# Sixteen adjacency-mask pieces moved from the first projection into the first attention of a four-layer graph network

## The chip, the cores and the metric

The kernel runs on one core of one Trainium2 chip. A core has a matrix engine (TensorE, PE in the profile, with its weight loads as PEld), a vector engine (VectorE, DVE), an activation engine (ScalarE, ACT), a general engine (GpSimd, POOL) and a queue engine (SyncE, SP). Each of them [...] waits on semaphores for the others. Transfers between the memory of the chip and the core's SBUF are issued by SP, ACT or POOL. The metric is the device time of one execution in microseconds (us), and the median of several executions is compared.

## The reference

The input is x, 3327 rows of 512 numbers, and adj, a 3327 x 3327 integer matrix of zeros and ones. Four layers follow one another, each closed by `x = layernorm(x + layer(x, adj))`. Layers 0, 2 and 3 are graph attentions. For a head with projected rows `Wh` and two scalars per row, f1 and f2,

```
e         = leaky_relu(f1[:, None] + f2[None, :], 0.2)
attention = softmax(where(adj > 0, e, -9e15), axis=-1)
h_prime   = attention @ Wh
```

Layers 0 and 2 have 8 heads of 64, layer 3 has 4 heads of 128. Layer 1 takes, for each row, the mean over its first 64 neighbours and two linear maps. The matrix adj is the same in all four layers.

## The kernel before

The rows are cut into NT = 26 tiles of 128 (NP = 3328), and the columns of the attention (the rows i that are being computed) into two halves of 1664. The adjacency matrix is given transposed. It is turned once into a mask of 8-bit floats that stays in SBUF for all four layers: `mask[:, t, i]`, one row tile t of neighbours against all i. This is done in 104 pieces of 128 x 832, four per row tile: q = 0 and 1 cover the first half of i, q = 2 and 3 the second. A piece is a transfer of 416 KB of integers into a buffer `raw` (L628) and one instruction that compares it with zero: on VectorE a `tensor_scalar` (L639), or on ScalarE a steep sigmoid (L638). `pieces` (L1103) lists first q = 0, 1 for every tile, then q = 2 for every tile, then q = 3.

The first stage is the projection of layer 0 (L1132 to L1154). For each row tile t, the rows of x are loaded (`xt`, issued on POOL after the first three), PE turns them (L266, four transposes), ScalarE copies the result out, and PE multiplies it with the weights (L276, 16 instructions into two PSUM banks `pw`, of which each has two buffers). VectorE then sums the turned rows (L268) and scales the product into `vt` (L282), which releases the PSUM bank and is stored to memory by POOL (L288). In this loop the mask is begun as well: `msteps` (L1105) is a list of steps for the first EARLY = 68 pieces, with eight `raw` buffers, eight loads on the queue of ScalarE and the rest on SP, and a lag of five steps between loading a piece and setting it. Three or four of these steps are taken per row tile (L1143). All 68 are set by VectorE.

The second stage is the attention of layer 0. It consists of 8 units: two halves times four slots s of two heads each. A unit goes over the 26 row tiles j. For each j and each of its two heads, VectorE makes `t` (L410, 128 x 1664), ScalarE makes `y` from it (L413), and PE multiplies `t` with the values `vj` (L433, 16 instructions per j) and, two tiles later and for two tiles at once, `y` and the mask with small matrices for the denominators (L385). There are six buffers of `t` and seven of `y`. Once per j two lists are served (L438 to L441): `background`, which holds the leftovers of the unit before (transposes L461 of its result) and jobs such as the neighbour counts (`count_jobs`, L658) or the small products `pa` of the later layers' weights (L1122); and `aside`, which holds the steps of the remaining mask pieces: load one, set the one before. The pool for these has two `raw` buffers, and the loads go through SP. In the kernel before, the 36 pieces that remain take 37 steps, so the first unit and eleven tiles of the second. ScalarE sets those with k % 5 in (1, 3), which are 14; VectorE sets 22.

The second half of the mask is first needed by the neighbour counts of the second half, in the third unit (half 0, s = 2), and by the attention from the fifth unit on. The instructions of PE stand in the order of the program. Those of the other engines are put in order by a scheduler, except for single ones that are pinned; the mask instructions of the attention are pinned.

Of the kernel before, what the change touches and what calls it, by code (L numbers as in the profile page):

```python
# [32 lines left out]
def kernel(  # L33
# [12 lines left out]
    NT = (N + P - 1) // P  # L46
# [575 lines left out]
    def mask_load(pool, t, q, eng):  # L622
        n = P if t < NT - 1 else LAST
        i0 = q * QW
        w_ = min(QW, N - i0)
        raw = pool.tile([P, QW], I32, name="raw")
        for a, z in _row_pieces(n):
            eng.dma_start(out=raw[a:z, :w_], in_=adjT[t * P + a:t * P + z, i0:i0 + w_])  # L628
        return raw

    def mask_set(raw, t, q, on_act=False):
        n = P if t < NT - 1 else LAST
        i0 = q * QW
        w_ = min(QW, N - i0)
        dst = mask[:n, t, i0:i0 + w_]
        if on_act:

            return nc.scalar.activation(dst, raw[:n, :w_], AF.Sigmoid, bias=below0[:n], scale=400.0, saturate=False)  # L638
        return nc.vector.tensor_scalar(dst, raw[:n, :w_], 0.0, None, op0=ALU.is_gt, saturate=False)  # L639


    def mask_steps(pool, pieces, lag, on_act, pinned, ahead=0):
        held = []

        def step(k):
            if k < len(pieces):
                held.append(mask_load(pool, *pieces[k], nc.scalar if k < ahead else nc.sync))
            if k >= lag:
                ins = mask_set(held[k - lag], *pieces[k - lag], on_act=(k - lag) in on_act)
                if pinned:  # L650
                    tc.keep_in_program_order(ins)
                held[k - lag] = None

        return [lambda k=k: step(k) for k in range(len(pieces) + lag)]
# [3 lines left out]
    def count_jobs(pool, half):  # L658
        jobs = []
        for s0, n in QUADS:  # L660
            i0, w_ = (half * HALF + s0) * P, n * P
            held = {}

            def counts(lo, hi, i0=i0, w_=w_, held=held):
                if lo == 0:
                    held["p"] = qp.tile([P, 4 * P], F32, name="pct", tag="q")
                for t in range(lo, hi):
                    g = t % 4
                    nc.tensor.matmul(held["p"][32 * g:32 * g + 32, :w_], onecol[:, 31 - t:63 - t],  # L669
                                     mask[:, t, i0:i0 + w_], start=t < 4, stop=t >= NT - 4)  # L670


            def none(i0=i0, w_=w_, held=held):
                ct = pool.tile([P, 4 * P], BF, name="ct", bufs=1)
                nc.scalar.copy(ct[:, :w_], held["p"][:, :w_])
                pn = qp.tile([P, 4 * P], F32, name="pn", tag="q")
                nc.tensor.matmul(pn[:, :w_], below, ct[:, :w_], start=True, stop=True)
                nc.vector.tensor_scalar(ct[:, :w_], pn[:, :w_], 128.0, None, op0=ALU.min)
                nc.sync.dma_start(out=ctd[:, i0:i0 + w_], in_=ct[:NT + 1, :w_])
                nb = pool.tile([P, 4 * P], F8, name="nb", bufs=1)  # L680
                nc.vector.tensor_scalar(nb[:, :w_], ct[:, :w_], 0.0, None, op0=ALU.is_equal, saturate=False)
                nc.sync.dma_start(out=mask[P - 1:P, NT - 1, i0:i0 + w_], in_=nb[NT:NT + 1, :w_])

            jobs += [lambda f=counts: f(0, NT), none]
        return jobs
# [401 lines left out]
    L0, L2, L3 = Layer(0, 8, False), Layer(2, 8, True), Layer(3, 4, True)  # L1087
# [3 lines left out]
    with tc.tile_pool(name="col0", bufs=1) as cp, tc.tile_pool(name="raw", bufs=2) as rawp, \  # L1091
            tc.tile_pool(name="at_r0", bufs=3, reuse_waits="tile") as rp:
        L0.columns(cp)
        L0.more_columns(cp)
        L0.piece_columns(cp)
        with tc.tile_pool(name="p_w", bufs=1, reuse_waits="tile") as wp, \
                tc.tile_pool(name="p", bufs=3, reuse_waits="tile") as pp, \
                tc.tile_pool(name="p_r", bufs=8, reuse_waits="tile") as rw0, \
                tc.tile_pool(name="p_ps", bufs=2, space=PSUM, reuse_waits="tile") as ps:
            if LAST < P:  # L1100
                nc.gpsimd.memset(mask[:, NT - 1, :], 0.0)
            nc.gpsimd.memset(mask[:, :, N:NP], 0.0)
            pieces = [(t, q) for t in range(NT) for q in range(2)] + [(t, q) for q in (2, 3) for t in range(NT)]  # L1103
            EARLY = 5 * NT // 2 + 3
            msteps = mask_steps(rw0, pieces[:EARLY], 5, (), False, 8)  # L1105

            def load(t):
                xt = pp.tile([P, F], F32, name="xt", bufs=5)
                load_tile(xt, x, t, nc.sync if t < 3 else nc.gpsimd)
                return xt  # L1110


            def attend(pool, tag, dst, wT, a, k, held):
                H = a.shape[1] // 2
                wt = pool.tile([P, F], F32, name="wt", tag=tag, bufs=FC if tag == "wt" else 1)
                nc.scalar.dma_start(out=wt, in_=wT[k * P:(k + 1) * P, :])
                if k == 0:
                    held["a"] = pool.tile([P, FC, 2 * H], F32, name=f"asb{H}", bufs=1)
                    nc.scalar.dma_start(out=held["a"], in_=a.rearrange("(c p) m -> p c m", p=P))
                    held["p"] = qp.tile([P, FC, 2 * H], F32, name="pa", tag="q")  # L1120
                for c in range(FC):
                    nc.tensor.matmul(held["p"][:, c, :], wt[:, c * P:(c + 1) * P], held["a"][:, k, :],  # L1122
                                     start=k == 0 and c == 0, stop=k == FC - 1,
                                     skip_group_check=True)
                if k == FC - 1:
                    nc.vector.tensor_copy(dst, held["p"] if len(dst.shape) == 3 else
                                          held["p"].rearrange("p c (e h) -> p c e h", e=2))

            def bank(e):
                return ps.tile([P, 512], F32, name=f"pw{e}")  # L1130

            xT = L0.project1(pp, ps, load(0), 0)  # L1132
            held = {}
            wsb = wp.tile([P, FC, 2, FW + L0.H], F32, name="wsb")
            for k in range(FC):
                attend(pp, "wt", wsb[:, :, :, FW:], w0T, a0, k, held)
            load_wide(wsb, w0, nc.scalar)
            pend = (xT, 0)
            for t in range(1, NT):
                xT = L0.project1(pp, ps, load(t), t)  # L1140
                L0.project2(pp, bank, wsb, *pend)
                pend = (xT, t)
                for _ in range(3 + t % 2):  # L1143
                    if msteps:
                        msteps.pop(0)()
                if t == HALF + 1:
                    L0.prepare(pp, 0)
                    L0.cut(pp, 0)
                if t == NT - 6:
                    L0.first_rows = L0.rows(rp, 0, 0)  # L1150
            L0.project2(pp, bank, wsb, *pend)
            for f in msteps:
                f()
            L0.mean(pp, bank, wsb)  # L1154

        def first_jobs(pool, half, s):

            if (half, s) == (0, 0):
                return [lambda: None] * 2 + [lambda: L0.prepare(f0, 1, "xr", 1, True), lambda: L0.cut(f0, 1, "h", 2, True)] + \
                    count_jobs(pool, 0)  # L1160
            if (half, s) == (0, 2):
                return count_jobs(pool, 1)
            if (half, s) == (0, 1):
                jobs = []
                for li, wT, a in ((2, w2T, a2), (3, w3T, a3)):
                    held = {}
                    jobs += [lambda k=k, li=li, wT=wT, a=a, held=held:
                             attend(f0, "xr", wa[li], wT, a, k, held) for k in range(FC)]
                return jobs
            return []  # L1170


        pieces = pieces[EARLY:]
        ends = []
        L0.attention(rp, first_jobs, mask_steps(rawp, pieces, 1, [k for k in range(len(pieces)) if k % 5 in (1, 3)], True),
                     ending=lambda sp: ends.extend(finish(f0, x, L0, 0, 2, 2, nc.sync, None, sp)))

    with tc.tile_pool(name="col2", bufs=1) as cp:
# [60 lines left out]
```

## Time and profile before

| what | value |
|---|---|
| median of three runs | 3378.35 us (3377.11 to 3380.59) |
| the profiled execution's own time | 3378.99 us |
| span of that execution (first to last instruction) | 3377.3 us |
| PE busy | 3252.0 us, 96% |
| DVE busy | 2687.1 us, 80% |
| ACT busy | 2358.2 us, 70% |
| read from and written to memory | 212.01 MB and 69.17 MB |
| end of the last product of the first projection | 142.2 us |
| last mask piece set in the first attention | 303.0 us |

The span is what the engines' records cover. The own time lies 1.69 us above it. A busy share is a mean over stages with different limits, and the records of PE count a pipelined matmul as busy while it waits for its place, so an engine that is 96% busy over the whole need not be what sets the end of a given stage.

### The profile page before, as it was taken

How to read it: one execution, taken by the hardware profiler on the slowest of the kernel's cores; microseconds unless marked ns; L12 is line 12 of the kernel's file. 1: busy time of each engine (PE TensorE's matmuls, PEld its weight loads, DVE VectorE, ACT ScalarE, POOL GpSimd, SP SyncE). 2: the span in 40 equal slices, each digit the busy share in tenths (PEclk: the TensorE clock that was granted, in tenths of full speed). 3: DMA queues.
4: the chain of work that ended last, by engine and by line, in shares of the span. 5: the costliest groups of instructions: out<-in, count | busy, mean ns of one | idle time of the engine just before them, and what ended most of it. 6: DMA issues, size and time to landing. Idle time of an engine off the chain costs nothing.

```text
span 3377.3 us, 47143 instructions
## 1 busy us (share of the span) xinstructions
PE 3252.0 (96%) x18424; PEld 1627.4 (48%) x18476; DVE 2687.1 (80%) x2619; ACT 2358.2 (70%) x2145; POOL 239.6 (7%) x389
## 2 busy tenths in 40 slices
PE   8799999999989999999989999999998999999997
PEld 7544344444444455545544444444446754455443
DVE  6799999999977544444449999999998766668887
ACT  2398998999953333333338999999997755558985
POOL 3100000000010111111110000000002000010110
PEclk9999999999999999999999999999998999999998
DMA  9544111110143433333320111111117411122311
GB/s 379 212 128 124 49 49 38 55 50 28 45 133 123 143 96 86 89 82 88 81 73 22 45 49 50 51 48 47 35 31 240 156 41 41 43 50 79 96 41 49
DMA packets 288014, 284.29 MB, mean 84 GB/s; under 512 B 107492, under 2 KB 223534, under 8 KB 287791
## 3 DMA queue, kind: packets, MB, share of 16 engines
q1 hardware_dynamic: 254063, 170.62, 16.7%
q0 software_dynamic: 28208, 102.96, 9.5%
q10 hardware_dynamic: 5520, 7.69, 0.7%
q8 instruction: 146, 2.39, 0.3%
q14 instruction: 77, 0.63, 0.1%
HBM read 212.01 MB, written 69.17 MB: 83 GB/s over the span
## 4 chain that ended last, share of the span: by engine, by line
PE 81%; DVE 5%; DMA 5%; issue 5%; ACT 4%; POOL 0%; SPq 0%; POOLq 0%; DVEq 0%; ACTq 0%
PE po L433 49%; PE acc L869 12%; PE pd L385 7%; PE pw L276 4%; DMA raw<-in_adjT_dram 3%; DVE t L410 3%; PE pz L737 3%; PE pi L740 2%; ACT y L413 1%; PE pk L829 1%; PE pt L461 1%; DMA h<-hd 1%; PE pa L1122 0%; DMA dd<-red 0%; PE pct L669 0%
## 5 line engine op out<-in xcount | busy, mean ns | idle before, releaser
L410 DVE SCALAR_TENSOR_TENSOR t<-rb,qc,mask 128x1664 f32<-128x1664 f32 x1040 | 1960.2, 1954 | 169.4 <-PE po L433 147.9
L413 ACT ACTIVATE y<-t,bi,sc 128x1664 fp8e4<-128x1664 f32 x1040 | 1770.5, 1768 | 309.5 <-PE pd L385 292.3
L433 PE MATMUL po<-t,vj 128*64 128x448 f32 (+3 forms) x8320 | 1908.6, 520 | 22.5 <-DVE t L410 19.8
L433 PEld LDWEIGHTS po<-t,vj 128*64 128x64 f32 (+1 forms) x8320 | 838.7, 148 | 970.4 <-issue 702.3
L869 PE MATMUL acc<-zs,kt 128*128 128x512 bf16 x1312 | 393.8, 381 | 2.2 <-issue 0.2
L276 PE MATMUL pw<-wsb,xT 128*128 128x264 f32 (+1 forms) x1248 | 300.2, 395 | 15.3 <-DVE vt L282 13.1
L869 PEld LDWEIGHTS <-kt 128*128 128x128 fp8e4 x2002 | 196.5, 98 | 242.1 <-issue 8.6
L821 ACT CAST pk<-cy 128x512 f32<-128x512 bf16 x169 | 99.1, 588 | 278.2 <-DVE kt L833 267.0
L385 PE MATMUL pd<-y,sden 128*32 128x448 fp8e4 (+1 forms) x4160 | 259.4, 341 | 10.4 <-ACT y L413 10.4
L276 PEld LDWEIGHTS pw<-wsb,xT 128*128 128x128 f32 x1248 | 239.8, 196 | 60.2 <-issue 10.6
L869 PE MATMUL acc<-zl,kt 128*128 128x512 bf16 x638 | 242.4, 380 | 0.6
L385 PEld LDWEIGHTS <-sden 128*32 128x32 bf16 x4160 | 117.5, 96 | 162.6 <-issue 139.8
L833 DVE SCALAR_TENSOR_TENSOR kt<-pk,mask 128x512 fp8e4<-128x512 f32 x169 | 116.1, 688 | 95.8 <-PE pk L829 95.8
L282 DVE TENSOR_TENSOR vt<-pw,dc 128x256 f32<-128x256 f32 x156 | 59.1, 418 | 147.4 <-ACT dc L277 142.7
L364 POOL DMA_DIRECT2D rb<-r x40 | 21.4, 534 | 1668.2 <-DVE t L410 1653.8
L280 ACT COPY rc<-pw 128x8 f32<-128x8 f32 (+1 forms) x78 | 12.7, 163 | 155.6 <-PE pw L276 155.6
L737 PE MATMUL pz<-wn,xT 128*128 128x512 f32 x208 | 95.8, 604 | 1.6 <-ACT xT L731 1.6
L841 DVE SCALAR_TENSOR_TENSOR y<-acc,cnt,bnb 128x512 f32<-128x512 f32 x26 | 19.5, 750 | 96.9 <-PE acc L869 89.5
L705 POOL DMA_DIRECT2D cy<-ctd x91 | 68.1, 748 | 385.5 <-ACT pk L821 312.8
L740 PE MATMUL pi<-wl,xT 128*128 128x512 f32 x208 | 93.5, 592 | 0.0
L639 DVE TENSOR_SCALAR mask<-raw 128x832 fp8e4<-128x832 int32 (+2 forms) x90 | 54.7, 615 | 39.7 <-DMA raw<-in_adjT_dram 39.2
L154 ACT ACT_TABLE_LOAD x46 | 59.0, 1283 | 37.3 <-DVE mv L153 36.7
(187 smaller groups left out, 1704.7 us busy)
## 6 DMA issues: line engine op xcount, KB each, us to landing
vj<-v SPq DMA_DIRECT2D x312, 128.0 KB
rb<-r POOLq DMA_DIRECT2D x40, 832.0 KB, 4.6
raw<-in_adjT_dram SPq DMA_DIRECT2D x67, 416.0 KB
cy<-ctd POOLq DMA_DIRECT2D x78, 256.0 KB, 4.0
h<-hd SPq DMA_DIRECT2D x61, 256.0 KB
v<-vt SPq DMA_DIRECT2D x50, 256.0 KB
hd<-hb SPq DMA_DIRECT2D x48, 256.0 KB
xr<-x POOLq DMA_DIRECT2D x45, 256.0 KB, 3.1
```

The source lines that it names most:

```text
L276: nc.tensor.matmul(pw[e][:, :FW + H], xT[:, c, :], wsb[:, c, e, :], start=c == 0, stop=c == FC - 1)
L282: nc.vector.tensor_tensor(vt[:, hs, :], pw[e][:, :FW].rearrange("p (h d) -> p h d", d=D), self.dc[:, t, hs].rearrange("p (h e) -> p h e", e=1)
L385: nc.tensor.matmul(pd[c][32 * kk:32 * kk + 32, :w_], lhsT, rhs, start=(kk, c) not in seen, skip_group_check=final is not None, stop=last a ...
L410: nc.vector.scalar_tensor_tensor(t, rb[k], self.qc[:, j, h:h + 1], mask[:, j, i0:i0 + IW], op0=ALU.max, op1=ALU.mult)
L413: nc.scalar.activation(y, t, AF.Sigmoid, bias=self.bi[:, j, h:h + 1], scale=self.sc[:, j, h:h + 1], saturate=False)
L433: nc.tensor.matmul(po[c][k * D:(k + 1) * D, :z - a_], vj[:, j % 2, k * D:(k + 1) * D], ts[k][:, a_:z], start=j == 0, stop=j == NT - 1)
L705: nc.gpsimd.dma_start(out=cy[:, :n, :], in_=ctd[t:t + n, b * GW:(b + 1) * GW] .rearrange("(o t) i -> o t i", o=1).to_broadcast([P, n, GW]))
L737: nc.tensor.matmul(pz, xT[:, c, :], wn[:, c, :], start=c == 0, stop=c == FC - 1)
L740: nc.tensor.matmul(pi, xT[:, c, :], wl[:, c, :], start=c == 0, stop=c == FC - 1)
L821: nc.scalar.copy(pks[k % 2], carry[b, t // 4 * 4][:, t % 4:t % 4 + 2, :])
L833: nc.vector.scalar_tensor_tensor(kt, pk, NEIGHBOURS, mask[:, t:t + 2, i0:i0 + GW], op0=ALU.is_le, op1=ALU.mult, saturate=False)
L869: nc.tensor.matmul(acc, kts[t][:, s * P:(s + 1) * P], zs(t, c) if c < 2 else zl[:, t, :], start=t == 0 and c == 0, stop=t == NT - 1 and c ...
```

## The change

EARLY falls from 68 to 52, which is exactly the pieces of the first half (q = 0 and 1). The steps taken per row tile in the projection fall from three or four to two or three. The other 52 pieces are set in the first attention, one per row tile, which takes 53 steps: all of the first two units and the first tile of the third. ScalarE sets those with k % 9 in (1, 3, 5, 7), which are 23, and VectorE sets 29. Four empty jobs are put ahead of the second half's neighbour counts.

```
-            EARLY = 5 * NT // 2 + 3
+            EARLY = 2 * NT
             msteps = mask_steps(rw0, pieces[:EARLY], 5, (), False, 8)
...
                 pend = (xT, t)
-                for _ in range(3 + t % 2):
+                for _ in range(2 + (t % 3 == 1)):
                     if msteps:
                         msteps.pop(0)()
...
             if (half, s) == (0, 2):
-                return count_jobs(pool, 1)
+                return [lambda: None] * 4 + count_jobs(pool, 1)
...
         pieces = pieces[EARLY:]
         ends = []
-        L0.attention(rp, first_jobs, mask_steps(rawp, pieces, 1, [k for k in range(len(pieces)) if k % 5 in (1, 3)], True),
+        L0.attention(rp, first_jobs, mask_steps(rawp, pieces, 1, [k for k in range(len(pieces)) if k % 9 in (1, 3, 5, 7)], True),
                      ending=lambda sp: ends.extend(finish(f0, x, L0, 0, 2, 2, nc.sync, None, sp)))
```

More of the change, by code (lines that the diff above doesn't have):

```diff
@@ L1103 @@
             pieces = [(t, q) for t in range(NT) for q in range(2)] + [(t, q) for q in (2, 3) for t in range(NT)]
-            EARLY = 5 * NT // 2 + 3
+            EARLY = 2 * NT
             msteps = mask_steps(rw0, pieces[:EARLY], 5, (), False, 8)
@@ L1142 @@
                 pend = (xT, t)
-                for _ in range(3 + t % 2):
+                for _ in range(2 + (t % 3 == 1)):
                     if msteps:
@@ L1161, in first_jobs @@
             if (half, s) == (0, 2):
-                return count_jobs(pool, 1)
+                return [lambda: None] * 4 + count_jobs(pool, 1)
             if (half, s) == (0, 1):
@@ L1174 @@
         ends = []
-        L0.attention(rp, first_jobs, mask_steps(rawp, pieces, 1, [k for k in range(len(pieces)) if k % 5 in (1, 3)], True),
+        L0.attention(rp, first_jobs, mask_steps(rawp, pieces, 1, [k for k in range(len(pieces)) if k % 9 in (1, 3, 5, 7)], True),
                      ending=lambda sp: ends.extend(finish(f0, x, L0, 0, 2, 2, nc.sync, None, sp)))
```

## The prediction

> **What bounds the kernel now.** The change touches two stages, so I looked for what ends last in each. First the busy table by stretches (us of the stretch, then busy time and instructions of PE, PEld, DVE, ACT, POOL, then PE clock, DMA share, GB/s):
>
> ```profile
> 100.00:120.00 20.00, 15.37 (x75) 12.82 (x74) 8.20 (x17) 3.33 (x14) 4.59 (x8) 1.00 1.02 396
> 120.00:140.00 20.00, 17.66 (x85) 14.69 (x84) 10.83 (x25) 4.64 (x20) 3.28 (x6) 1.00 0.47 178
> ...
> 204.00:256.00 52.00, 48.68 (x353) 22.45 (x347) 51.95 (x38) 49.45 (x32) 0.75 (x2) 1.00 0.47 140
> 303.00:360.00 57.00, 56.93 (x435) 27.73 (x433) 55.95 (x34) 47.51 (x29) 1.03 (x2) 1.00 0.21 64
> ```
>
> The late projection is full on the DMA engines (share 1.02) while PE and DVE have room. The attention is the reverse: DMA is half empty and DVE is busy 51.95 of 52 us.
>
> Next the waits of the projection (0 to 142 us) and PE's instructions in order of time, with start, length and the idle time before:
>
> ```profile
> DVE mask L639 <- DMA raw<-in_adjT_dram: 38.5, 37, 2.8
> PE pw L276 <- DVE vt L282: 12.4, 9, 3.0
> ```
>
> ```profile
> 95.55 3.73 PE L276 MATMUL pw<-wsb,xT 128*128 128x264 f32 x16
> 99.55 3.73 PE L276 MATMUL pw<-wsb,xT 128*128 128x264 f32 x16
> 103.55 3.73 PE L276 MATMUL pw<-wsb,xT 128*128 128x264 f32 x16
> ...
> 109.29 3.80 PE L276 MATMUL pw<-wsb,xT 128*128 128x264 f32 x16 [1.58 <-DVE vt L282]
> ...
> 116.57 3.80 PE L276 MATMUL pw<-wsb,xT 128*128 128x264 f32 x16 [3.05 <-DVE vt L282]
> ...
> 138.61 3.62 PE L298 MATMUL pw<-wsb,xm 128*128 128x256 f32 x16
> ```
>
> Undisturbed, PE takes one row tile per 4.00 us (95.55, 99.55, 103.55). From 104 us on it does not: it waits for `vt`, which stands on DVE behind mask pieces whose transfer has not landed. The chain is transfer, L639, L282, PE.
>
> Last, what DVE waited for in the whole first attention, 142 to 936 us, and its pace (view in order of time):
>
> ```profile
> DVE t L410 <- ACT y L413: 1.6, 4, 0.6
> DVE t L410 <- PE po L433: 1.5, 3, 0.6
> DVE t L410 <- PE pw L298: 1.0, 1, 1.0
> DVE mask L639 <- DMA raw<-in_adjT_dram: 0.8, 2, 0.5
> DVE t L410 <- DMA v<-ms: 0.5, 1, 0.5
> ```
>
> ```profile
> 276.53 0.59 DVE L639 TENSOR_SCALAR mask<-raw 128x831 fp8e4<-128x831 int32 x1
> 277.03 3.81 DVE L410 SCALAR_TENSOR_TENSOR t<-rb,qc,mask 128x1664 f32<-128x1664 f32 x2
> ...
> 303.46 18.71 DVE L410 SCALAR_TENSOR_TENSOR t<-rb,qc,mask 128x1664 f32<-128x1664 f32 x10
> ```
>
> These waits sum to 5.4 us in 794: DVE sets the pace there. A mask piece costs it 0.50 us (277.03 - 276.53; the record of 0.59 overlaps the next), a `t` 1.86 us (18.71 less the 0.09 overlap, over 10), so 3.72 us per row tile without masks.
>
> **What the Trainium skill says.** "TensorE: Matmul & The Clock Gate", its opening table, gives VectorE, ScalarE and GpSimd strictly in-order queues; the trace agrees, since `vt` waits behind a mask piece that it has nothing to do with. "DMA: Bandwidth & Descriptors", section "Issuing engines are not separate DMA queues", says that transfers of all issuing engines interleave on the same 16 DMA engines; here SP's pieces and POOL's `xt` and `vt` fill one share of 1.02. Its "Specifications" put the fabric's ceiling at 435 GB/s, and 396 is moved. "ScalarE: Activation LUTs", section "What ACT_TABLE_LOAD costs", gives an activation with a bias operand 280 ns + 0.833 ns per element, 973 ns for 832; the trace has 982.
>
> **The change part by part.**
>
> *Pieces taken out of the projection: -7.5 to -8.5 us, taken as -8.0.* In the built instruction order, DVE, SP, ACT and POOL are the same as before up to the pieces set near 80 us; then the sixteen pieces that the old order set from 97.3 to 126 us are gone and nothing takes their place. From the product starting at 95.55, nine row tiles remain: 9 x 3.56 + 8 x 0.44 (transposes) = 35.6 us, so the product L298 starts at 131.1 instead of 138.61: 7.5 us. Something may come in ahead of it: the product at 91.48 waited 1.96 us for a `vt` that DVE reached after reciprocals, casts and pieces; one of these pieces now stands behind that `vt`, with a short transfer wait: up to 1.0 us, taken as 0.5. Against it: the last two early loads now stand behind ScalarE's `r` stores on SP; they have about 8 us until needed, and a piece takes about as long at full DMA share. If they are late by one step, 1 to 2 us are lost. Sixteen pieces of 416 KB are 6.8 MB, 17 us of DMA at 396 GB/s, so the remaining `xt` loads and `rb` broadcasts find room. Before 80 us nothing changes, and those waits stay.
>
> *Pieces put on DVE in the attention: +3.5 us.* 29 instead of 22, 7 x 0.50. DVE has no idle time to hide them in except this: in the second unit (303 to 340 us) the products `pa` lengthen PE's row tile to about 4.5 us (310.27 to 337.38 for six tiles), DVE runs ahead until buffers run out, and then stops 0.6 and 0.2 us. The new pieces fall into this stretch and take up that room: -0.8.
>
> *Pieces put on ACT: 23 instead of 14, 9 x 0.88 (pitch from 217.77 to 218.65) = 7.9 us, counted as nothing.* Seven of the nine fall after step 37, in the stretch where ACT is busy 47.51 of 57 us and waits for PE's L385; per row tile it then has 2 x 1.69 + 0.39 = 3.8 us against DVE's 4.0. Without that cover ACT would hold `t` buffers and DVE would wait, up to about 5 us.
>
> *New waits of DVE and ACT for transfers: +1.0, between 0 and 5.* There are two `raw` buffers, and a load starts only when the piece before in its buffer is set. A load also stands in SP's queue behind `vj` loads that wait for PE. Before, this cost DVE 0.8 us over 22 pieces. Now 16 further steps run while PE is up to two row tiles behind. Behind a late piece on DVE stand the `t` of all later tiles; behind one on ACT stand the `y`, and at the end of the first unit one copy of the result (L453), since the built order puts a mask piece ahead of the last of the four. PE waits for that copy, but has a row tile of `t` in store.
>
> *Counts moved four jobs later: 0.* The same 104 matmuls, casts and stores, later in the same unit, beside the same `t` and `y`. The last piece is set at that unit's first tile, well ahead of them.
>
> Sum: -8.0 + 3.5 - 0.8 + 1.0 = -4.3 us. DVE's delay or gain passes through to the end of the attention, and the later stages keep their order, so it passes to the end. Span 3377.3 becomes 3373.0, and the profiled execution's 3378.99 becomes 3374.7; against the median shown (0.64 lower) the forecast is 3374.0. That is 0.13%, inside the 0.2% (6.8 us) which a measurement of this kernel can tell from no change.
>
> **The rivals.**
>
> A, the attention swallows the pieces: if PE's and ACT's own limits leave DVE more room than its 5.4 us of waits show, the seven cost 0 to 1 us, and 8 us of gain stand alone: 3370.4. For it: PE is busy 56.93 of 57 us beside them. Against it: DVE's records touch one another.
>
> B, the projection gives less: PE's last tiles wait for something else, such as `xt` loads that stand on POOL behind `vt` stores and `rb` broadcasts (12.3 us from issue to landing), or a lowered PE clock (1.76 us for one product at 55.98 us, 5.49 instead of 3.73). With half of the gain, -4 + 3.5: 3378.
>
> C, slower: the two `raw` buffers. Where ACT empties a buffer that DVE's next piece needs, DVE waits for ACT's backlog and for a transfer; a load issued at 256.07 us landed 7.9 us later, beside a new unit's `rb` broadcasts, and a step lasts 4.0. The new pattern has five such handovers, and nine DVE pieces now meet PE's and ACT's backlog in the second unit. With 1 us on each of nine and 1.5 on five: 16 us less the 4.3: 3390. It decides the sign at 4.3 us of new waits and the measured verdict from about 11. Against it: before, seven handovers cost 0.8 us together.
>
> That the change doesn't do what it says can be set aside: the built order has the 16 pieces out of the projection, and 29 and 23 in the attention.
>
> **How the numbers follow.** Forecast 0.48, its own range 3371 to 3378; A 0.18; B 0.20; C 0.14. Faster by over 0.2% (under 3371.6): most of A and the low edge of the forecast, 0.21. Slower by over 0.2% (above 3385.1): C and a little of B, 0.15. Same: 0.64. The range takes A whole and B, the unknown waits up to about +5 and a clock step, and leaves out most of C: 3368 to 3384.
>
> **What would show it.** Right: the product L298 starts near 130.6 us, no wait of PE for `vt` after 95 us, DMA share well under 1 from 100 us; 29 and 23 mask pieces in the attention, DVE's waits there still about 5 us, the first attention ending about 4 us earlier. Wrong: L298 later than 134 us (B); DVE waits for `raw` above 4 us in the attention, or `t` waiting for `y` (C); a second unit no longer than before (A).

## The result

The changed kernel takes 3374.21 us (median of 20 runs, 3371.16 to 3377.05) against 3378.82 us (3373.42 to 3383.62, 20 runs) of the kernel before on the same chip: a ratio of 0.9987 with a 95% interval of 0.9981 to 0.9993, so 4.6 us faster by the medians and 4.4 by the ratio, between 2.4 and 6.4. The forecast was 3374.0. The profiled execution has a span of 3371.2 us, 6.1 less than before; only 2.7 of these lie in the two stages that the change touches, and the last section takes up the others.

The same stretches as before (us of the stretch, then busy time and instructions of PE, PEld, DVE, ACT, POOL, then PE clock, DMA share, GB/s), of the changed kernel:

```profile
100.00:120.00 20.00, 20.00 (x102) 17.19 (x101) 7.22 (x15) 4.92 (x20) 5.08 (x10) 1.00 0.63 233
120.00:140.00 20.00, 16.08 (x75) 12.96 (x73) 9.92 (x18) 7.58 (x19) 2.68 (x5) 0.97 0.23 75
204.00:256.00 52.00, 49.34 (x364) 21.92 (x362) 52.00 (x35) 50.60 (x37) 1.12 (x2) 1.00 0.51 150
303.00:360.00 57.00, 56.16 (x426) 26.98 (x427) 55.44 (x38) 49.82 (x33) 1.05 (x2) 1.00 0.51 159
```

In the projection the DMA share fell from 1.02 to 0.63 and PE went from 15.37 to 20.00 busy us of 20. In the second unit DMA is no longer at 0.21 but at 0.51, and DVE is as full as it was.

PE's products in order of time, changed kernel (start, length, idle time before in brackets where there is any):

```profile
92.31 3.80 PE L276 MATMUL pw<-wsb,xT 128*128 128x264 f32 x16 [0.73 <-ACT xT L267]
96.38 3.73 PE L276 MATMUL pw<-wsb,xT 128*128 128x264 f32 x16
...
124.38 7.29 PE L276 MATMUL pw<-wsb,xT 128*128 128x264 f32 x32
131.50 3.62 PE L298 MATMUL pw<-wsb,xm 128*128 128x256 f32 x16
```

From 96 us on every row tile takes 4.00 us, without a bracket. L298 starts at 131.50 instead of 138.61.

What DVE waited for from 133 to 936 us, changed kernel:

```profile
DVE t L410 <- PE po L433: 3.5, 6, 0.8
DVE mask L639 <- DMA raw<-in_adjT_dram: 1.3, 2, 0.8
DVE t L410 <- DMA v<-ms: 1.0, 1, 1.0
DVE t L410 <- PE pw L298: 1.0, 1, 1.0
DVE t L410 <- ACT y L413: 0.7, 2, 0.5
```

These are 7.5 us instead of 5.4. The rise is in the first line, 3.5 instead of 1.5: DVE has run ahead and waits for PE to give back a `t` buffer. Only 0.4 of it lies in the second unit; 1.6 lies in the first row tiles of the third (0.74 and 0.84 us, at 368.68 and 371.48 us). PE in turn has a wait that it did not have before (waits of PE, 133 to 960 us):

```profile
PE pa L1122 <- DMA wt<-in_w2T_dram: 2.7, 2, 2.4
```

`wt` are the weights of the eight small products of the second unit. ScalarE issues their loads, and now issues them between its mask pieces. The last run of 30 products of the first attention, before and then in the changed kernel:

```profile
945.43 5.80 PE L433 MATMUL po<-t,vj 128*64 128x448 f32 x30 [0.82 <-DVE t L410]
```

```profile
942.75 5.80 PE L433 MATMUL po<-t,vj 128*64 128x448 f32 x30 [0.82 <-DVE t L410]
```

It starts 2.7 us earlier. So of the 7.1 us won by L298, the attention gave back 4.4. From the first `t` of one unit to the first of the next, the second unit grew from 103.2 to 107.1 us and the third from 100.9 to 102.8; the first shrank by 0.4.

### The profile page after: what moved, and what is told of

The parts are those of the page before. It is cut to its first block, busy times and chain, and to the rows that moved or that the text cites. A ratio compares the mean times of both kernels' runs of the same rounds, so it can differ in the third digit from the quotient of the medians.

```text
span 3371.2 us, 47193 instructions
## 1 busy us (share of the span) xinstructions
PE 3252.1 (96%) x18476; PEld 1627.2 (48%) x18476; DVE 2681.5 (80%) x2610; ACT 2364.6 (70%) x2154; POOL 238.2 (7%) x389
## 4 chain that ended last, share of the span: by engine, by line
PE 86%; DVE 6%; DMA 3%; ACT 3%; issue 2%; SPq 0%; ACTq 0%; POOL 0%; DVEq 0%; POOLq 0%
PE po L433 52%; PE acc L869 12%; PE pd L385 7%; PE pw L276 6%; DVE t L410 3%; PE pz L737 3%; PE pi L740 2%; ACT y L413 1%; PE pk L829 1%; PE pt L461 1%; DMA raw<-in_adjT_dram 1%; PE pt L266 0%; DMA h<-hd 0%; PE pt L729 0%; PE pa L1122 0%
## 5 line engine op out<-in xcount | busy, mean ns | idle before, releaser
L869 PE MATMUL acc<-zs,kt 128*128 128x512 bf16 x1352 | 401.3, 381 | 0.0
L639 DVE TENSOR_SCALAR mask<-raw 128x832 fp8e4<-128x832 int32 (+3 forms) x81 | 49.4, 619 | 27.0 <-DMA raw<-in_adjT_dram 27.0
```

Of the source, the lines that this page charges most:

```text
L869: nc.tensor.matmul(acc, kts[t][:, s * P:(s + 1) * P], zs(t, c) if c < 2 else zl[:, t, :], start=t == 0 and c == 0, stop=t == NT - 1 and c ...
```

## The experiments

One theory and two disputes stand behind the runs. The theory: the projection is held up by the transfers of the sixteen pieces, and the attention is paced by VectorE, so that a piece costs its time there. The disputes are whether it is the transfers or the setting that costs in the projection, and what a piece costs in the attention beside its 0.50 us on VectorE. The median of the kernel before lay between 3377.5 and 3380.2 us from one set of runs to the next, so each kernel is compared by its ratio to the runs of before that it shared. A difference of two medians from different sets is only a rough figure beside it.

### The attention alone

The projection of before (68 pieces) with the attention of after:

```
-        pieces = pieces[EARLY:]
+        pieces = pieces[2 * NT:]
```

together with the changed lines for the split and the counts, and with EARLY and the steps per row tile left at their old values.

> The projection of the kernel before (68 pieces set there) with the attention of the changed kernel (all 52 second-half pieces loaded and set, 29 on VectorE and 23 on ScalarE, the counts four jobs later). Sixteen pieces are set twice, to the same values. My theory, that VectorE sets the pace of the attention and that every one of the seven pieces more costs 0.50 us there beside some new waits: L298 starts near 138.6 us as before, VectorE's waits in the attention stay at 6 to 9 us, the attention ends 4 us later than in the kernel before, and the time is 3378.8 + 4.3 = 3383 us. Rival, that the attention swallows the pieces and the missing gain lies in the differences of single executions: 3379 us, the attention's end as before.

Measured: 3382.23 us, ratio 1.0011 (1.0004 to 1.0018): 3.5 us slower by the medians, 3.7 by the ratio. In the order of PE, L298 and then the last run of products:

```profile
140.22 3.62 PE L298 MATMUL pw<-wsb,xm 128*128 128x256 f32 x16
...
953.56 5.80 PE L433 MATMUL po<-t,vj 128*64 128x448 f32 x30 [0.81 <-DVE t L410]
```

That stage takes 953.56 - 140.22 = 813.3 us; in the kernel before 945.43 - 138.61 = 806.8. The attention does not swallow the pieces.

### The sets without the transfers

The kernel before, with pieces 52 to 67 of the projection set from data that lies in SBUF already:

```
-            if k < len(pieces):
+            if k >= loads:
+                held.append(held[loads - 3])
+            elif k < len(pieces):
...
-            msteps = mask_steps(rw0, pieces[:EARLY], 5, (), False, 8)
+            msteps = mask_steps(rw0, pieces[:EARLY], 5, (), False, 8, 2 * NT)
```

> The kernel before, but the last sixteen pieces of its projection are not loaded: VectorE sets them from a piece that lies in SBUF already (so the mask holds wrong values in those sixteen pieces). All VectorE instructions stay, sixteen transfers of 416 KB go. My theory, that the transfers and not VectorE's work delay the last row tiles: L298 starts at 131 to 132 us instead of 138.6, no wait of PE for vt after 95 us, the DMA share from 100 us falls below 1, and the time is 3378.8 - 7 = 3371.8 us. Rival, that VectorE's sixteen extra instructions of 0.5 us ahead of vt are the cause: L298 stays above 136 us and the time is 3377 to 3379 us.

Measured: 3370.73 us, ratio 0.9978 (0.9970 to 0.9986): 8.05 us faster by the medians, 7.4 by the ratio. The stretch in the projection and L298:

```profile
100.00:120.00 20.00, 20.00 (x102) 17.15 (x101) 12.40 (x27) 4.93 (x20) 11.15 (x16) 1.00 0.74 257
```

```profile
96.81 3.73 PE L276 MATMUL pw<-wsb,xT 128*128 128x264 f32 x16
...
131.96 3.62 PE L298 MATMUL pw<-wsb,xm 128*128 128x256 f32 x16
```

VectorE is busier there than in either kernel (12.40 of 20 us), and PE still runs without a gap. So sixteen sets ahead of `vt`, with nothing to wait for, cost nothing that can be seen here; the sixteen transfers bring the loss. L298 comes 6.65 us earlier than in the kernel before, so nearly all of the gain lies in the projection. The two halves add up: by the ratios -7.4 and +3.7 make -3.7, against -4.4 for the change. That the medians, -8.05 and +3.45, make the measured -4.6 to the digit is luck, with halves that are uncertain by some 2.5 us each.

### The split between VectorE and ScalarE

Three kernels differ from the changed one in a single expression, which pieces ScalarE sets: none, every second (26), two of three (35).

```
-k % 9 in (1, 3, 5, 7)
+False            (none)
+k % 2            (26)
+k % 3 < 2        (35)
```

> The changed kernel with all 52 pieces of the attention on VectorE and none on ScalarE. My theory, that VectorE sets the pace of the attention and ScalarE has room: 23 more pieces of 0.50 us on VectorE, +11.5 us less up to 1 us of waits: 3374.2 + 11 = 3385 us, with VectorE's waits in the attention at 4 to 8 us. Rival, that ScalarE's pieces and the handover of the two raw buffers between the engines cost as much as VectorE's: the waits of VectorE for y, raw and products fall away, and the time is within 3 us of the changed kernel, 3372 to 3377 us.

> The changed kernel with every second piece of the attention on ScalarE: 26 and 26 instead of 23 on ScalarE and 29 on VectorE. With 29 pieces on VectorE the time was 3374.2 us, with 52 it was 3380.7, with 17 it was 3381.1. If the slope of 0.50 us per piece still holds at 26, 3374.2 - 1.5 = 3372.7 us. Rival, that ScalarE is at its limit already with 23: 3376 us, with VectorE's waits in the attention above 9 us.

> The changed kernel with two of three pieces of the attention on ScalarE (35 instead of 23) and 17 instead of 29 on VectorE. My theory, that VectorE alone sets the pace: 12 pieces x 0.50 = 6 us gained, 3368 us, if ScalarE keeps up. Rival, that ScalarE becomes the bound: it is busy 50.60 of 52 us in the first unit already, and twelve pieces more of 0.88 us are 10.6 us, of which the first unit's part finds no room: VectorE then waits for y by several us, and the time is 3373 to 3378 us.

Measured: none 3380.7 us, ratio 1.0003 (0.9995 to 1.0011); 26: 3375.27 us, ratio 0.9993 (0.9985 to 1.0001); 35: 3381.07 us, ratio 1.0006 (0.9998 to 1.0014). The split of 23, with its 0.9987, is the best of these four. With none on ScalarE, VectorE in order of time:

```profile
209.30 0.58 DVE L639 TENSOR_SCALAR mask<-raw 128x832 fp8e4<-128x832 int32 x1
209.80 3.81 DVE L410 SCALAR_TENSOR_TENSOR t<-rb,qc,mask 128x1664 f32<-128x1664 f32 x2
213.53 0.58 DVE L639 TENSOR_SCALAR mask<-raw 128x832 fp8e4<-128x832 int32 x1
```

A row tile takes 213.53 - 209.30 = 4.23 us, the 3.72 of two `t` and 0.50 of a piece, and nothing between. VectorE's waits in the attention of that kernel are all of these:

```profile
DVE t L410 <- DMA v<-ms: 1.1, 1, 1.1
DVE mask L639 <- DMA raw<-in_adjT_dram: 0.5, 1, 0.5
DVE t L410 <- PE pw L298: 0.5, 1, 0.5
DVE t L410 <- PE po L433: 0.4, 1, 0.4
```

That is 2.5 us instead of 7.5. Of the 23 x 0.50 = 11.5 us that were added to VectorE, 5.0 came back as waits that fell away, so 6.5 us should be left. The median rose by 6.5 us; by the ratios it is 5.4, and by the stage from L298 to the last run of products 5.3. With 35 on ScalarE, the waits of VectorE and then of PE:

```profile
DVE t L410 <- PE po L433: 10.9, 9, 4.1
DVE mask L639 <- DMA raw<-in_adjT_dram: 2.9, 4, 1.1
```

```profile
PE pd L385 <- ACT y L413: 9.4, 9, 1.8
...
PE pa L1122 <- DMA wt<-in_w2T_dram: 4.0, 1, 4.0
```

ScalarE is late with `y`, PE waits for `y` and for the weights that ScalarE issues, VectorE waits for PE. With the small lines the waits are 16.5 us. Two of them, 4.1 and 2.5 us long, come while PE's clock is low. One of the products `pa` with 35 pieces on ScalarE, and the stretch around it:

```profile
303.24 1.72 PE L1122 MATMUL pa<-asb,wt 128*128 128x16 f32 x8 [3.98 <-DMA wt<-in_w2T_dram]
```

```profile
300.00:310.00 10.00, 6.76 (x24) 3.33 (x24) 6.53 (x4) 9.28 (x7) 0.00 (x0) 0.67 0.64 194
```

The same product in the changed kernel, where the granted clock of that stretch is 1.00:

```profile
303.53 1.07 PE L1122 MATMUL pa<-asb,wt 128*128 128x16 f32 x8 [2.36 <-DMA wt<-in_w2T_dram]
```

PE waits for `wt`, and behind that wait its clock is 0.67 and the product takes 1.72 instead of 1.07 us; then VectorE waits 4.1 us for PE. The wait of 2.5 us stands in the same way behind a stretch of 0.66 (250 to 260 us).

So a piece on ScalarE is not free: in these executions 23 pieces go with 5.0 us of waits, 0.22 each, and the next 12 with 9.0 us, 0.75 each, of which a good part is PE's clock. On VectorE a piece costs 0.50. ScalarE's pieces are not all that delays `wt`: with none on ScalarE, PE still waits 1.5 us for it. The 52 pieces bring transfers into the second unit too (DMA share 0.51 instead of 0.21), and no run separates the two.

### The small products out of the way

The eight products `pa` and the loads of `wt` moved to the fourth unit, in the changed kernel and, as a control, in the kernel before:

```
-            if (half, s) == (0, 1):
+            if (half, s) == (0, 3):
```

> The changed kernel with the eight small products pa (L1122) and the loads of their weights wt moved from the second unit to the fourth, where no mask pieces are set. In the changed kernel PE waits 2.7 us for wt in the second unit, whose loads ScalarE issues and now issues between its mask pieces, just where PE is the late engine; VectorE then waits 3.5 us for PE. My theory, that this is where the attention lost more than 0.50 us per piece: both waits go or fall under 1 us, the stages from L298 to the attention's end take 2 to 3 us less than in the changed kernel (813.0 us), and the time is 3374.2 - 2.5 = 3371.7 us. Rival, that the loss is VectorE's pieces alone and the products cost the same wherever they stand: 3374 us.

> The control to the run before it: the kernel before with the same eight products moved to the fourth unit. In the kernel before PE does not wait for wt, since only pieces up to the twelfth row tile of that unit are set there. My theory: no gain, 3378.8 within 1.5 us. Rival, that the products are better placed in the fourth unit whatever the pieces do: 2 to 3 us faster here too, 3376 us.

Measured: changed kernel 3374.3 us, ratio 0.9989 (0.9981 to 0.9998); kernel before 3381.74 us, ratio 1.0008 (1.0000 to 1.0016). PE's waits for `wt` are gone in the changed kernel, and DVE's waits for `po` fell:

```profile
DVE mask L639 <- DMA raw<-in_adjT_dram: 1.7, 2, 1.1
DVE t L410 <- PE po L433: 1.7, 3, 0.6
```

But the sum of VectorE's waits went only from 7.5 to 6.6, the stage from L298 to the last run of products from 811.25 to 810.09 us, and the time did not fall. (The 813.0 us of the expectation counts the same stage to the end of the last `t`.) The theory of this pair fell: the wait for `wt` is real, and taking it away alone pays at most 1 us. The rival fits, that the products cost about the same wherever they stand: moved in the changed kernel, they take 2.0 us from the second unit (107.1 to 105.1) and add 2.8 to the fourth (96.9 to 99.7); in the kernel before it is 2.2 and 2.9.

### Spread out over four units

Three steps of the mask in five row tiles, the counts a unit later, with the split of the change and with 31 pieces on ScalarE:

```
+        def spread(steps):
+            return [g for k, f in enumerate(steps) for g in ([f, lambda: None] if k % 3 else [f])]
...
-            if (half, s) == (0, 2):
+            if (half, s) == (0, 3):
```

with `spread(...)` around the list of steps, and in the second kernel `k % 5 in (1, 2, 4)` for ScalarE.

> The changed kernel with the 53 steps of the mask in the attention spread out: three steps in five row tiles instead of one in each, so they fill three units and eleven row tiles of the fourth; the counts of the second half go to the fourth unit. The split (29 on VectorE, 23 on ScalarE) is the same. The attention's time has so far been VectorE's work plus its waits, and with no piece on ScalarE the waits were 2.5 us instead of 7.5. My theory, that ScalarE's pieces cost waits only where they come so densely that ScalarE has no time to catch up: the waits of VectorE in the attention fall from 7.5 to 3 to 4 us and the time is 3374.2 - 4 = 3370 us. Rival, that a piece costs its share of waits wherever it stands, as the products pa did: 3374 us, waits 7 us.

> As the run before it, spread out, and with 31 pieces on ScalarE and 21 on VectorE. If ScalarE's pieces are free once they are spread, eight pieces of 0.50 us less on VectorE: 4 us under the spread kernel, 3366 us. Rival, that ScalarE, with 3.38 us for the two y of a row tile and 0.6 x 0.6 x 0.88 = 0.32 us for pieces, is again too near to VectorE's 3.84 us together with its copies: waits above 8 us in the attention, 3371 to 3375 us.

Measured: 3379.12 us, ratio 0.9996 (0.9988 to 1.0005), and 3375.27 us, ratio 0.9989 (0.9982 to 0.9995). VectorE's longest waits in the first:

```profile
DVE t L410 <- PE po L433: 5.6, 4, 3.5
DVE t L410 <- ACT y L413: 3.6, 6, 1.5
```

With the small lines they are 11.3 us, more than the theory and the rival expected. One wait of 3.5 us makes the difference: just before it PE waits 3.6 us for `wt`, and from 300 to 310 us its clock is 0.66. Without that wait 7.8 us are left, no fewer than the 7.5 of the dense order. So the spread bought nothing in waits, and the theory fell.

The second kernel, against the first, has eight pieces fewer on VectorE, waits of 11.5 instead of 11.3 us, and a stage from L298 to the last run of products that is 3.3 us shorter. Spread out, eight more pieces on ScalarE cost next to nothing, as the theory had it; the waits above 8 us are those of its rival. Its ratio of 0.9989 is no better than the change's.

### More out of the projection, and back into it

Three kernels move eight pieces: out of the projection (EARLY 44, two steps per row tile), back into it between the last `vt`, and back into it behind the last `vt`.

```
-            EARLY = 2 * NT
+            EARLY = 2 * NT - 8                                           (out)
+            EARLY = 2 * NT + 8                                           (back, between)
...
-                for _ in range(2 + (t % 3 == 1)):
+                for _ in range(2):                                       (out)
+                for _ in range(2 + (t % 3 == 1 or t > 15)):              (back, between)
...
-            for f in msteps:
+            for f in msteps + mask_steps(rw0, pieces[EARLY:EARLY + 8], 7, (), True):   (back, behind)
```

In the kernel that takes them out, the counts stand eight and two jobs later; in the one that sets them behind, the attention's list begins at EARLY + 8.

> The changed kernel with eight pieces more taken out of the projection (EARLY is 44, two steps per row tile), so 60 in the attention, 33 of them on VectorE and 27 on ScalarE. In the projection of the changed kernel PE still waits 4.2 us for vt before 93 us. My theory: these eight pieces save less there than the sixteen did, at most the 4.2 us; L298 starts at 128 to 131 us; in the attention they cost 4 x 0.50 on VectorE and about 4 x 0.75 on ScalarE, 5 us: 3375 to 3379 us. Rival, that every piece taken out saves 0.5 us in the projection and costs 0.22 to 0.25 us in the attention, as the sixteen did: 3374.2 - 2 = 3372 us.

> The changed kernel with eight of the sixteen pieces back in the projection, but taken with its last row tiles (EARLY is 60, three steps per row tile from the seventeenth on); 44 remain for the attention, 24 of them on VectorE. My theory, that in the projection only a full DMA share costs time: eight pieces are 3.3 MB, 8.4 us at 396 GB/s, and from 100 us the changed kernel leaves 37% and then 77% of the DMA engines idle, so L298 starts within 1.5 us of the changed kernel's 131.5; in the attention five pieces of 0.50 us go: 3374.2 - 2.5 + 1 = 3372.7 us. Rival, that VectorE's vt waits behind late pieces as soon as pieces stand there: L298 at 135 us, half of the gain gone, 3375 to 3376 us.

> The changed kernel with eight pieces more in the projection, as in the run with eight back, but all eight are set behind the last vt of VectorE, and loaded when buffers come free (EARLY stays 52, then eight with a lag of seven behind the loop); 44 remain for the attention, 24 of them on VectorE. With eight back between the vt, L298 started at 136.36 us instead of 131.50, with the DMA engines full until 115 us. My theory, that the transfers harm only through the set that stands ahead of a vt on VectorE: L298 starts at 130 to 132 us, the stage from there to the last products of the attention takes 809 us as in that run, 2 us less than in the changed kernel, and the time is 2 us under the changed kernel's, 0.9981 of the kernel before. Rival, that the eight transfers hold up the xt loads beside them whatever VectorE does: PE waits for xT, L298 at 134 us or later, and no gain over the changed kernel.

Measured: out 3374.44 us, ratio 0.9983 (0.9977 to 0.9990); between 3375.43 us, ratio 0.9993 (0.9987 to 1.0000); behind 3373.82 us, ratio 0.9984 (0.9974 to 0.9993). None is clearly better than the change's 0.9987.

*Out* has L298 at 131.07 us, at the upper end of the 128 to 131 expected of the first theory and within the spread of the kernels that share the change's projection (129.96 to 131.91): these eight save nothing that can be seen there. Its attention is 2.5 us longer than the change's. Its time should then have been some 2 us longer, and its ratio is 0.9983 against 0.9987; with the intervals as they are, that stays open. *Between* has it at 136.36, five of the seven us lost again with half of the pieces. PE and then VectorE in that kernel:

```profile
111.48 5.49 PE L276 MATMUL pw<-wsb,xT 128*128 128x264 f32 x16 [3.03 <-DVE vt L282]
...
136.36 3.62 PE L298 MATMUL pw<-wsb,xm 128*128 128x256 f32 x16
```

```profile
102.88 0.59 DVE L639 TENSOR_SCALAR mask<-raw 128x832 fp8e4<-128x832 int32 x1 [2.42 <-DMA raw<-in_adjT_dram]
103.39 0.75 DVE L282 TENSOR_TENSOR vt<-pw,dc 128x256 f32<-128x256 f32 x2
...
108.29 0.59 DVE L639 TENSOR_SCALAR mask<-raw 128x832 fp8e4<-128x832 int32 x1 [1.80 <-DMA raw<-in_adjT_dram]
110.41 0.59 DVE L639 TENSOR_SCALAR mask<-raw 128x832 fp8e4<-128x832 int32 x1 [1.52 <-DMA raw<-in_adjT_dram]
110.92 0.75 DVE L282 TENSOR_TENSOR vt<-pw,dc 128x256 f32<-128x256 f32 x2
```

`vt` comes at 103.39 and then only at 110.92, since three late pieces stand ahead of it. PE waits 3.03 us for it, and its next product takes 5.49 us instead of 3.73, at a clock of 0.66 (111 to 116 us): together 4.8 of the 4.9 us lost. My expectation had read the 37% of idle DMA off a stretch of 20 us. Cut into halves, the stretch of the changed kernel reads differently:

```profile
100.00:110.00 10.00, 10.00 (x53) 8.65 (x52) 4.33 (x9) 2.79 (x11) 4.00 (x8) 1.00 1.02 376
110.00:120.00 10.00, 10.00 (x51) 8.54 (x50) 2.89 (x6) 2.13 (x9) 1.08 (x2) 1.00 0.23 89
```

Until 110 us there is no room at all. *Behind* moves as much from 100 to 110 us (410 GB/s, against 412 in *between*), and PE loses no step:

```profile
131.11 3.62 PE L298 MATMUL pw<-wsb,xm 128*128 128x256 f32 x16
```

The transfers were felt here too: `vt` comes at 103.83, 108.94 and 115.35 us, once after 3.57 us of waiting for a store of `vt`. But PE, which has two buffers of each bank, took that without a wait. What cost 4.9 us in *between* is the late set ahead of `vt`. The Trainium skill gives VectorE a strict first-in-first-out queue ("TensorE: Matmul & The Clock Gate", opening table), and the trace of *between* agrees: the sets that wait 1.5 to 2.4 us hold up the `vt` behind them. VectorE at the end of the projection in *behind*:

```profile
131.52 0.76 DVE L282 TENSOR_TENSOR vt<-pw,dc 128x256 f32<-128x256 f32 x2 [2.80 <-ACT dc L277]
132.20 4.12 DVE L639 TENSOR_SCALAR mask<-raw 128x832 fp8e4<-128x832 int32 x8
...
137.83 7.54 DVE L410 SCALAR_TENSOR_TENSOR t<-rb,qc,mask 128x1664 f32<-128x1664 f32 x4
```

Here the eight sets stand ahead of the first `t`, which is 6.7 us behind L298; in the kernel before and in the changed one it is 3.65 (142.26 and 138.61, 135.15 and 131.50). VectorE sets the pace again, and of the 4 us for eight pieces 3 have only been moved: the stage takes 812.4 us, not the 809 expected, and no gain over the change is to be seen.

### What all fourteen kernels say together

For each: the pieces that VectorE sets in the attention (for "behind", with the eight ahead of its first `t`), its waits there on `t`, `mask` and `wa`, the stage from the start of L298 to the start of the last run of products, what is left of it when 0.50 us per piece and the waits are taken off, VectorE's longest single wait for PE in it, and the clock granted to PE from 295 to 320 us, where in most of the kernels the first products `pa` wait for `wt`.

| kernel | pieces | waits, us | stage, us | left, us | longest for PE, us | clock |
|---|---|---|---|---|---|---|
| before | 22 | 5.4 | 806.8 | 790.4 | 0.6 | 1.00 |
| after | 29 | 7.5 | 811.3 | 789.3 | 0.8 | 1.00 |
| attention alone | 29 | 9.2 | 813.3 | 789.6 | 1.8 | 0.86 |
| sets without transfers | 22 | 4.9 | 805.0 | 789.1 | 0.6 | 1.00 |
| none on ScalarE | 52 | 2.5 | 816.6 | 788.1 | 0.4 | 1.00 |
| 26 on ScalarE | 26 | 9.7 | 812.6 | 789.9 | 2.3 | 0.86 |
| 35 on ScalarE | 17 | 16.5 | 815.2 | 790.2 | 4.1 | 0.86 |
| products moved | 29 | 6.6 | 810.1 | 789.0 | 0.6 | 1.00 |
| before, products moved | 22 | 5.8 | 806.3 | 789.5 | 0.6 | 1.00 |
| spread | 29 | 11.3 | 815.6 | 789.8 | 3.5 | 0.86 |
| spread, 31 on ScalarE | 21 | 11.5 | 812.3 | 790.3 | 3.7 | 0.86 |
| eight more out | 33 | 7.7 | 813.8 | 789.6 | 1.9 | 0.86 |
| eight back, between | 24 | 7.4 | 809.2 | 789.8 | 0.6 | 0.93 |
| eight back, behind | 32 | 7.1 | 812.4 | 789.3 | 2.1 | 0.86 |

The stages differ by 11.6 us, what is left by 2.3. By itself this is bookkeeping: the work and the waits of any engine add up to the stage. That VectorE sets the pace is shown by the size of its waits, 2.5 to 16.5 us in more than 800, and by the kernel with none on ScalarE, where 23 more pieces on VectorE make the stage 5.3 us longer though its waits fall by 5.0. (A straight line through the fourteen, the stage less the waits against the pieces, gives an estimate of 0.44 us per piece, a little under the 0.50 read from the starts.)

The last two columns go together. In the seven kernels with a clock of 0.86 VectorE's longest wait for PE is 1.8 to 4.1 us, in the other seven at most 0.8. In each of the seven it comes behind a wait of PE for `wt` of 2.3 to 4.0 us. The two kernels with the same attention, after and attention alone, differ in this: 7.5 and 9.2 us of waits, with a longest of 0.8 and 1.8. So part of what the kernels differ by is PE's clock and not the price of a piece. That PE's wait lowers the clock was not tried by itself, and its length alone does not tell: after 2.36 us the clock stayed at 1.00 (after), after 2.33 and 2.40 us it did not (attention alone, eight more out).

## Why the prediction was right

*The projection, -8.0.* Right in its cause, and in its size with some luck. The kernel with the sets but without the transfers measures it as -8.05 us by medians and -7.4 by the ratio (-4.7 to -10.1). L298 came at 131.50 instead of the 131.1 computed and the 130.6 named as the sign. The working has a slip and a hope that failed. From 95.55 only seven groups of transposes follow, not eight, since the last two products run without one between them: 9 x 3.56 + 7 x 0.44 = 35.1 us, which is what the changed kernel takes from 96.38 to 131.50, and alone would have been a gain of 7.9. And the 0.5 that might come in ahead did not: the product that started at 91.48 starts at 92.31, with a wait of 0.73 us for `xT` in place of 1.96 for `vt`. Two early loads behind ScalarE's stores were not late. The 7.1 us between the two profiled executions are not exact either: L298 starts at 138.61, 140.22 and 141.47 in the three with the projection of before, and at 129.96 to 131.91 in the seven with that of the change, 9.1 us apart in the mean.

*Seven pieces on VectorE, +3.5.* Right: 29 and 23 pieces are set, at 0.50 us each. The -0.8 that stood beside it was wrong. The stops of the second unit are still there, 0.28, 0.61 and 0.39 us instead of 0.18 and 0.61.

*Nine pieces on ScalarE, counted as nothing.* This term was too small. Its cover was said to be the stretch in which ScalarE waits for PE. But that is the stretch in which PE is late, and what ScalarE delays there delays PE. All of VectorE's waits together rose by 2.1 us, where -0.8 and +1.0 had left 0.2 for them. Most of the rise stands at the end of the second unit, on ScalarE, PE and VectorE of the changed kernel:

```profile
362.42 0.99 ACT L638 ACTIVATE mask<-raw,below 128x831 fp8e4<-128x831 int32 x1
363.31 1.71 ACT L453 COPY ob<-po 128x448 f32<-128x448 f32 x4
...
363.87 10.29 PE L433 MATMUL po<-t,vj 128*64 128x448 f32 x48 [0.83 <-ACT ob L453]
...
368.68 1.95 DVE L410 SCALAR_TENSOR_TENSOR t<-rb,qc,mask 128x1664 f32<-128x1664 f32 x1 [0.74 <-PE po L433]
```

A mask piece stands ahead of the four copies of the result. PE waits 0.83 us for them, its clock is 0.83 from 360 to 370 us, and VectorE gets its `t` buffers back 0.74 and 0.84 us late. The prediction knew this place, at the end of the first unit, and took a row tile of `t` in store as enough. Whether it costs depends on more than the piece: in the kernel with the attention alone PE waits 1.13 us for the same copies, keeps a clock of 1.00, and VectorE does not wait there. At the 0.22 us per piece of the kernel with none on ScalarE nine pieces cost 2.0 us. The prediction had named the price without cover as up to 5 us.

*New waits for transfers, +1.0.* VectorE's own waits for `raw` rose by 0.5 us, 0.8 to 1.3. The step had not looked at the weights `wt` among the transfers; PE waits 2.7 us for them, and the run without that wait shows at most 1 us for it.

*Counts moved four jobs later, 0.* No run tests this alone. The third unit, in which they stand, is 1.9 us longer; one mask piece more and VectorE's waits there, some 1.4 us more, account for that.

*The sum.* The forecast of +3.7 for the attention was measured as +3.5 by the medians of the kernel with the attention alone and +3.7 by its ratio (1.4 to 6.1), and as +4.4 and +6.5 by the stages of two single executions. By the table's terms it is 3.5 + 2.1 = 5.6. The intervals can't tell these apart, so the total of -4.3 against a measured -4.6 is right within what can be measured. That it is so near owes something to luck: the waits were some 2 us too small, and the projection may have given more than 8. The prediction took 0.13% to be too little to tell from no change; the interval of 0.9981 to 0.9993 tells it. The sign that the first attention ends about 4 us earlier came at 2.7, and that of about 5 us of waits at 7.5.

*The rivals.* A, that the attention swallows the pieces, is refuted by the kernel with the attention alone, which is slower than before, and by the second unit, which is 3.9 us longer. B, half of the gain in the projection, is refuted by L298. C put the danger in the two `raw` buffers and had the wrong place: waits for `raw` rose by 0.5 us. (Its sums take new waits off a total that held 1.0 us of them already; the sign would turn at 5.3 us, not at 4.3.) Its other half, ScalarE's and PE's backlog, is real but small at 23 pieces; with 35 it brings 9.0 us more of waits, PE's low clock among them, and uses the gain up (ratio 1.0006).

## What to carry to other kernels

Price a moved instruction on the engine that paces the new stage, and then again by what it delays on the engine beside it. Here ScalarE had idle time, but it was time spent waiting for a late PE, and part of what was put into it came back to VectorE by way of PE. A transfer in a full DMA stretch need not cost by itself: here eight of them cost 4.9 us with their sets ahead of `vt`, and no step of PE with their sets behind it. Read a DMA share in stretches no longer than the slack that is to be used, since a mean of 0.63 was 1.02 and 0.23. When two executions of the same stage differ, look at the granted clock of that stage before pricing the difference.

## What the runs showed of the hardware

Eight mask pieces in a row took 4.12 us on VectorE, 0.515 each, while a single one is recorded with 0.58 to 0.60; the records of back-to-back instructions overlap by about 0.09, so a sum must be made with distances between starts.

A wait of PE can cost more than its length. In *between*, 3.03 us of waiting for `vt` were followed by a product of 5.49 us instead of 3.73; in the attention, 3.98 us of waiting for `wt` by one of 1.72 instead of 1.07. In both the granted clock was 0.66 to 0.67 in the stretch around it.

Of the 6.1 us between the two profiled spans, 2.7 are there at the end of the first attention. At the first `t` of the second attention (1753.06 and 1747.47 us) it is 5.6: another 2.9 us arose in between, mostly in layer 1, in which nothing was changed. PE's clock is one place where the two executions differ: from 1480 to 1500 us it is 0.91 in the kernel before and 1.00 in the changed one. A clock of 0.91 there is (1 - 0.91) x 20 = 1.8 us of PE's full speed. That it makes the difference was not tried; differences of this size between single executions are why the parts of this change were weighed by medians and by the ends of stages.
